# A graph network's message kernel: a row table one iteration sooner, and casts moved behind a relu

## The chip, the cores and the metric

The kernel runs on one core of a Trainium2 chip. A core has five engines that each work through a queue of their own, in order: TensorE (PE: matmuls, and PEld: the loading of their stationary operand), VectorE (DVE), ScalarE (ACT), GpSimd (POOL) and SyncE (SP, which here issues the transfers).[...] The metric is the device time of one execution in microseconds (us). TensorE writes its results to PSUM[...].

## The reference

There are 128 graphs of 64 nodes with 128 features. Each ordered pair (i, j) of nodes of a graph has a message: a three-layer MLP on the two nodes' features, with relu and layer norm after the first and the second layer. The message is multiplied by the adjacency matrix, so only pairs joined by an edge count, and the messages of a node are summed. A second MLP of the same form, on the node's features and its sum, gives the update that is added to the features.

```python
pair_feats = jnp.concatenate([f_i, f_j], axis=-1)
messages = _mlp(pair_feats, msg_w0, msg_b0, ..., msg_w2, msg_b2)
messages = messages * coupling_matrix[..., None]
agg = jnp.sum(messages, axis=2)
upd_in = jnp.concatenate([part_feats, agg], axis=-1)
updated = part_feats + _mlp(upd_in, upd_w0, upd_b0, ...)
```

About one entry of the adjacency matrix in eight is 1, and the kernel works on the edges alone.

## The kernel before, in words

**Tiling.** Each graph gets 640 slots for edges (`CAP`). Two graphs make a *pair* p (64 pairs), eight graphs a *block* b (16 blocks, `PB` = 4 pairs each), four graphs a *quarter* q of 5 chunks (32 quarters). A *chunk* n is 512 slots (160 chunks, `NCHK`), 10 to a block.

**First layer.** The first layer of the message MLP is linear in the two nodes, so the kernel computes for each node its part as the first and as the second node once (`rows`: two matmuls per graph, with `w0a` and `w0b`, into one bank; four graphs are a *half* of a block). The result is split into a rounded part and the rest: `rows_hi` (L463, ACT) casts the bank to `abh`, `rows_lo` (L469, DVE) subtracts that from the bank and writes `abl`. The bank is free when `rows_lo` is done. For each edge slot a matrix of marks S says which two nodes it joins: its upper half comes from `node_rows` (an ACT cast for pairs 2 to 5, a POOL cast for later ones, L491 and L493), its lower half from `marks` on PE and `compare` on DVE; each half is put in its place by two transfers (`stack`, L500). `node_rows` and `marks` both read the mask `tp` that `make_tp` (L484, DVE) makes of a `distance` (L478, ACT). Then `layer0` (L535) multiplies `abl` and `abh` with S, and one relu with bias on ACT (L538) empties the bank `hps` into h. There is one bank `hps`, so the next chunk's matmuls wait for that relu.

**The rest.** `stats0` turns h on PE and takes its statistics on DVE (`bn_stats`, L548). Per quarter, POOL makes the variance of five chunks (`var0_of`: L245 to L249), ACT its root (`root_of`: L255, L562), PE turns it (`turn_root`, L568). `layer1` (L602, L605) runs eight iterations after `layer0`, then a relu, statistics, and the weighted sum over edges.

**Order of the work.** Nothing schedules at run time. The program is a loop over iterations n; for each, work is registered in named places by `at(n, place, function)`, and the loop runs the places in this order: "a", "m", `layer1`, "b", `layer0`, `stats0`, "k", `stats1`, "x", "x1", "x2", "e0", "e1", "e". Each engine gets its instructions in the order in which the loop meets them. So "a" is ahead of the chunk's relu on ACT and "x" behind it.

**Around the change.** In the first iterations the pipeline is filled. Before the loop chunks 0 to 2 are done by hand, iterations 0 and 1 do `layer0` of chunks 3 and 4, iterations 2 to 4 none, and from iteration 5 on each does its own chunk. Chunks up to 4 need only the first half of block 0's rows; chunk 5 is the first to need the second, `rows(0, 1)`. Meanwhile the weights of the later layers are derived (`derivation`): each is made by an "ahead" step on ACT (L177, L200), a product on PE in a borrowed bank (L180 to L212, places "x"), and a step that empties the bank an iteration later (L184 on DVE, L193 on ACT, place "m"). The product in iteration 2 is `b1b`, the shift of the second layer. In iteration 3 place "b" `bias_table` casts it on ACT (`b1hi`, L643), and POOL builds a table from it (L645 to L649). In the same iteration, in place "e0", POOL does `var0_of` of quarter 0, and in iteration 4, place "b", ACT its root.

Borrowed banks come from `ubank` (tile `mu`, one bank: derivation in iterations 1, 2, 4, 5, 6, 7, 9 and 10, and all `rows`) and from `abank` (tile `ma`, one bank: `turn_x` in iteration 0, `count` in 1, `turn_root` in 6).

Of the kernel before, what the change touches and what calls it, by code (L numbers as in the profile page):

```python
# [23 lines left out]
def tile_gnn(  # L24
# [52 lines left out]
    PB = 4  # L77
# [207 lines left out]
    def edge_path(es):  # L285
# [18 lines left out]
        def abank():  # L304

            return ps_a.tile([P, 512], F32, name="ma")

        def ubank():

            return ps_u.tile([P, 512], F32, name="mu")  # L310
# [13 lines left out]
        def at(n, place, fn, *args):  # L324
            plan.setdefault((n, place), []).append((fn, args))
# [117 lines left out]
        def rows(b, half, k0=0, k1=4):  # L443

            blk = blocks[b]
            ps = blk["ab_ps", half] if k0 else ubank()
            for k in range(k0, k1):
                s = slice((4 * half + k) * N, (4 * half + k + 1) * N)
                nc.tensor.matmul(ps[0:N, k * C:(k + 1) * C], lhsT=blk["xnT"][:, s], rhs=w0a,
                                 start=True, stop=True)  # L450
                nc.tensor.matmul(ps[N:P, k * C:(k + 1) * C], lhsT=blk["xnT"][:, s], rhs=w0b,
                                 start=True, stop=True)
            blk["ab_ps", half] = ps
# [354 lines left out]
        for b in range(NB):  # L808
            o = b * CPB
            if b > 1:  # L810
                at(max(o - 25, 0), "a", load_adj, b)
                at(max(o - 12, 0), "a", load_x, b)
            if b > 0:
                r = max(o - 12, 1)
                at(max(o - 14, 0), "m", rank, b)
                at(r, "x", count, b)
                at(r + 1, "a", count_out, b)
                at(r + 1, "a", degrees, b)
                at(max(o - 9, r + 1), "e", place, b)
                at(*((r + 2, "a") if b == 1 else (o - 7, "e")), place_out, b)  # L820
                at(max(o - 7, 13), "m", odd_weights, b)
                at(o - 3, "x", turn_x, b)
                at(o - 2, "a", turn_x_out, b)
            for half, n in ((0, o - 2), (1, o + 3)):
                if n >= 0:
                    at(n, "x2", rows, b, half)
                    at(n + 1, "a", rows_hi, b, half)
                    at(n + 1, "m", rows_lo, b, half)
        for b in reversed(range(NB)):
            o = b * CPB  # L830
            n = o + QC + SC
# [35 lines left out]
        for p in range(NP):  # L867
            n = p * TG * 2 // CH
            if p > 1:
                if p > 2:  # L870
                    at(max(n - 7, p - 2), "a", distance, p)
                    at(max(n - 6, p - 2), "m", make_tp, p)
                at(n - 5, "a", node_rows, p)
                at(n - 4, "a", stack, p, 0, IR)
                for k in range(2):
                    at(n - 5 + k, "k", marks, p, k)
                    at(n - 5 + k, "k", compare, p, k)
                at(n - 3, "a", stack, p, 1, JR)
            w = p // 2 * QC + QC + L1 + p % 2
            last = p // 2 == NQ - 1  # L880
            at(w - 4, "a", node_marks, p)
            q, h = divmod(p, 2)
            for g in range(2):
                wait = h + 2 if q == NQ - 3 else h + 1 if q == NQ - 2 else 2 + (2 * h + g + 1) // 2
                at(*((NCHK + L1, "b") if last else (q * QC + QC + L1 + wait, "e1")), weights, p, g)
            at(NCHK + L1 + 1 if last else q * QC + SC - (q >= NQ - 3), "x1", reduce, p)
        for q in range(NQ):
            n = q * QC + QC if q else LEAD
# [35 lines left out]
        place_rest()  # L924
        bias_rows()
        rows(0, 0, 0, 2)
        rows_hi(0, 0, 0, 2)

# [17 lines left out]

        marks_here(0)
        rows(0, 0, 2, 4)
        rows_here(0, 0)
        rows_here(0, 1)  # L950
# [97 lines left out]
    with ExitStack() as es:  # L1048
        es.enter_context(tc.manual_schedule())
        flag = edge_path(es)  # L1050
# [160 lines left out]
```

## Time and profile before

| what | value |
|---|---|
| time, median of 3 runs | 575.55 us (574.04 to 575.84) |
| span of the profiled execution | 573.7 us, mean granted TensorE clock 0.983 |
| PE busy | 549.3 us (96%) |
| PEld busy | 515.0 us (90%) |
| DVE busy | 479.8 us (84%) |
| ACT busy | 476.3 us (83%) |
| POOL busy | 339.6 us (59%) |
| PE busy in 20 to 25 and 25 to 30 us | 4.01 and 2.58 us of 5 |
| PE busy in 100 to 200 us | 100.00 us of 100 |
| PE granted clock in 10 to 15, 15 to 20, 20 to 25 us | 0.50, 0.62, 1.00 |

A row of a timeline gives the start and the duration of an instruction in us, engine, line, operation, what it writes and reads, and in brackets the idle time of its engine before it with the instruction that ended it. A busy time is of the engine as a whole over the span; the stages differ, and the change lies in the first 40 us of 574.

### The profile page before, as it was taken

What the parts mean: (1) busy time and instruction counts of PE and PEld (TensorE: products, weight loads), DVE (VectorE), ACT (ScalarE), POOL (GpSimd) and SP (SyncE); (2) the same over time, 40 slices, a digit from 0 to 9 for tenths busy, and PEclk for the clock granted to TensorE, in tenths of its full rate; (3) what the DMA queues carried; (4) which work ended last, traced back from release to release, by engine and by line L of the source; (5) the groups of instructions that cost most, each with busy time, mean ns of one, the idle gap of its engine ahead of it and who ended that gap; (6) DMA issues with size and microseconds to landing.
All of it is one profiled execution on the core that took longest, in us unless ns stands there. A gap on an engine that the chain in (4) does not pass through costs nothing. (4 is left out here: it accounts for less than half of the span.)

```text
span 573.7 us, 15753 instructions
## 1 busy us (share of the span) xinstructions
PE 549.3 (96%) x5303; PEld 515.0 (90%) x5303; DVE 479.8 (84%) x1944; ACT 476.3 (83%) x1149; POOL 339.6 (59%) x898
## 2 busy tenths in 40 slices
PE   6899899999999999999999999999999999989894
PEld 4687889999999999999999999999999999979883
DVE  5768788997979899797989889798989979786686
ACT  6788979998988889898888989898888989875434
POOL 3435566665657676575757666565767656545342
PEclk7899999999999999999999999999999999998998
DMA  4464645555465545457574545546475464531201
GB/s 101 102 146 114 133 105 133 101 134 111 103 153 111 134 96 142 113 113 128 125 134 110 138 109 130 105 111 154 102 128 108 125 115 109 114 93 30 35 21 41
DMA packets 90769, 63.21 MB, mean 110 GB/s; under 512 B 57398, under 2 KB 74812, under 8 KB 90684
## 3 DMA queue, kind: packets, MB, share of 16 engines
q1 hardware_dynamic: 90396, 62.03, 49.1%
q8 instruction: 43, 0.70, 0.5%
q14 instruction: 42, 0.34, 0.2%
q10 hardware_dynamic: 288, 0.13, 0.1%
HBM read 6.82 MB, written 4.19 MB: 19 GB/s over the span
## 5 line engine op out<-in xcount | busy, mean ns | idle before, releaser
L548 DVE BATCH_NORM_STATS2 st<-hT 128x6 f32<-128x128 f32 x640 | 141.9, 284 | 36.4 <-PE hT L544 34.8
L605 PE MATMUL z<-w1c,h 128*128 128x128 f32 x1280 | 172.2, 277 | 0.0
L605 PEld LDWEIGHTS z<-w1c,h 128*128 128x128 f32 x1280 | 161.2, 192 | 8.0 <-issue 5.1
L593 ACT ACTIVATE z<-b1b,m_sd 128x128 f32<-128x128 f32 x360 | 133.6, 371 | 8.7
L615 DVE BATCH_NORM_STATS2 st<-y 128x6 f32<-128x128 f32 x640 | 137.5, 277 | 2.7 <-ACT y L608 1.4
L608 ACT ACTIVATE y<-z 128x512 f32<-128x512 f32 x160 | 94.5, 591 | 26.2 <-PE z L605 24.5
L538 ACT ACTIVATE h<-hps,b0c 128x512 f32<-128x512 f32 x160 | 109.4, 684 | 3.6 <-PE hps L535 3.3
L544 PE MATMUL hT<-ident,h 128*128 128x128 f32 x640 | 98.2, 276 | 1.5 <-DVE st L548 1.5
L678 POOL TENSOR_TENSOR w<-oh,m_q 128x320 f32<-128x320 f16 x126 | 91.9, 741 | 9.9 <-PE hT L544 5.3
L535 PE MATMUL hps<-s,abl 128*128 128x512 f32 (+3 forms) x256 | 93.2, 376 | 3.7 <-ACT h L538 2.8
L544 PEld LDWEIGHTS hT<-ident,h 128*128 128x128 f32 x640 | 76.7, 142 | 12.0 <-ACT h L538 1.3
L493 POOL CAST i<-tp 128x640 fp32r<-128x640 f16 x58 | 41.6, 718 | 68.0 <-DVE tp L484 49.1
L535 PE MATMUL hps<-s,abh 128*128 128x512 f32 (+3 forms) x256 | 79.5, 329 | 0.0
L691 PE MATMUL ys<-y,w 128*64 128x128 f32 x1280 | 76.9, 275 | 0.0
L691 PEld LDWEIGHTS ys<-y,w 128*64 128x64 f32 x1280 | 69.2, 137 | 4.2 <-issue 3.6
L245 POOL TENSOR_TENSOR m_d<-st 128x20 f32<-128x20 f32 x62 | 16.3, 263 | 88.4 <-DVE st L548 76.7
L517 DVE TENSOR_TENSOR j<-mk,cmpt 128x320 fp32r<-128x320 f32 x124 | 58.6, 473 | 1.2 <-PE mk L509 1.2
L535 PEld LDWEIGHTS hps<-s,abl 128*128 128x128 f32 x256 | 50.0, 195 | 6.2 <-ACT h L538 4.5
L478 ACT ACTIVATE d<-slot,mid 128x640 f16<-128x640 f16 x64 | 52.7, 823 | 0.0
L535 PEld LDWEIGHTS hps<-s,abh 128*128 128x128 f32 x256 | 50.3, 197 | 0.0
L469 DVE TENSOR_TENSOR abl<-mu,abh 128x512 fp32r<-128x512 f32 (+1 forms) x33 | 22.3, 675 | 31.9 <-ACT abh L463 31.7
L509 PE MATMUL mk<-tp,posall 128*128 128x320 f16 x126 | 38.0, 301 | 1.1 <-DVE tp L484 0.9
(226 smaller groups left out, 978.2 us busy)
## 6 DMA issues: line engine op xcount, KB each, us to landing
s<-i SPq DMA_DIRECT2D x124, 160.0 KB, 2.7
s<-j SPq DMA_DIRECT2D x124, 160.0 KB, 2.6
xn<-in_x_dram SPq DMA_DIRECT2D x15, 256.0 KB, 3.6
out_dram<-uo SPq DMA_DIRECT2D x15, 256.0 KB, 2.4
an<-in_adj_dram SPq DMA_DIRECT2D x16, 128.0 KB, 2.7
oh<-tp SPq DMA_TRANSPOSE x64, 3.6
xn<-in_x_dram SPq DMA_DIRECT2D x2, 128.0 KB
out_dram<-uo SPq DMA_DIRECT2D x2, 128.0 KB, 2.6
```

The lines of the kernel that those rows point to most:

```text
L478: nc.scalar.activation(D[p], slot, AF.Abs, bias=blocks[b]["mid"][:, q:q + 1], scale=-1.0)
L517: nc.vector.tensor_tensor(JR[p][:, c], MK.pop((p, k))[:, 0:HC], cmpt[:, c], op=ALU.is_equal)
L535: nc.tensor.matmul(ps[:, c:c + w], lhsT=ab[:, g % 4, :], rhs=s, start=(k == 0), stop=(k == 1))
L538: nc.scalar.activation(H[n], ps, AF.Relu, bias=b0c)
L544: nc.tensor.transpose(ps[:, t, :], H[n][:, t * P:(t + 1) * P], ident)
L548: nc.vector.bn_stats(ST0[q][:, CH * c + t, :], ps[:, t, :])
L593: nc.scalar.activation(Z[n][:, t, :], W["b1b"], AF.Copy, scale=SR[q][:, k:k + 1])
L605: nc.tensor.matmul(ps[:, t, :], lhsT=h[:, t * P:(t + 1) * P], rhs=W["w1c"], start=False, stop=True, skip_group_check=True)
L608: nc.scalar.activation(Y[n], ps, AF.Relu)
L615: nc.vector.bn_stats(ST1[q][:, CH * c + t, :], Y[n][:, t, :])
L678: (nc.vector if p == NP - 2 else nc.gpsimd).tensor_tensor(WT[p][:, :, g, :], OH[p][:, :, g * N:(g + 1) * N], Q[q][:, k:k + TG].unsqueeze(2 ...
L691: nc.tensor.matmul(YS[b][g * N:(g + 1) * N, k, :], lhsT=w[:, t, g, :], rhs=y, start=(t == 0), stop=(t == TG - 1))
```

## The change

It has three parts. The second half of rows of block 0 moves from iteration 3 to iteration 2, and with it its `rows_hi` and `rows_lo` from iteration 4 to iteration 3; as `ubank` is taken by the derivation in iteration 2, it gets the bank `abank`, free in iterations 2 to 5. The purpose is that `abh` and `abl` are there well ahead of chunk 5, and that the derivation's bank is not held by them in iteration 4. Second, the casts of pairs 2 to 5 (`node_rows`) go from place "a" to place "x" of the same iterations (0, 2, 5 and 7), that is behind the chunk's relu. Third, the `distance` of pair 4 goes from "a" to "x" of iteration 3.

```diff
-            ps = blk["ab_ps", half] if k0 else ubank()
+            ps = blk["ab_ps", half] if k0 else abank() if (b, half) == (0, 1) else ubank()
...
-            for half, n in ((0, o - 2), (1, o + 3)):
+            for half, n in ((0, o - 2), (1, o + 3 if b else 2)):
...
+                early = "x" if p < PB + 2 else "a"
                 if p > 2:
-                    at(max(n - 7, p - 2), "a", distance, p)
+                    at(max(n - 7, p - 2), "x" if p == PB else "a", distance, p)
                     at(max(n - 6, p - 2), "m", make_tp, p)
-                at(n - 5, "a", node_rows, p)
+                at(n - 5, early, node_rows, p)
```

## The prediction

> **What bounds the kernel now.** I read the table of busy time by stretch first.
>
> ```profile
> 20.00:25.00 5.00, 4.01 (x36) 3.09 (x36) 3.81 (x16) 3.72 (x13) 4.08 (x8) 1.00 0.53 129
> 25.00:30.00 5.00, 2.58 (x14) 1.73 (x14) 3.68 (x7) 3.18 (x10) 4.14 (x9) 1.00 0.52 123
> ...
> 100.00:200.00 100.00, 100.00 (x998) 95.52 (x995) 87.47 (x356) 89.10 (x218) 63.65 (x168) 1.00 0.55 121
> ```
>
> The columns after the length are busy us of PE, PEld, DVE, ACT and POOL, then the granted clock and DMA. From 100 to 200 us (and alike to 500) PE has no pause and its weight loads fill 95.5% of the time: TensorE is the bound. The change touches only iterations 0 to 8, which run from about 15 to 37 us. There PE has 1.0 + 2.4 us of idle time between 20 and 30 us. Whatever starts PE's unbroken run at 30 us earlier or later moves the end by as much, because PE then (5.00 busy of 5.00 us from 30 to 35 and from 35 to 40) has no pause before 44.6 us, and the waits after that (0.8 us before the turn of the next quarter's root) are on work that PE's own output feeds.
>
> So I looked at what PE waits for in that stretch, in PE's timeline.
>
> ```profile
> 25.82 0.49 PE L180 MATMUL mu<-wg,mean_m 128*128 128x128 f32 x2 [1.41 <-DVE abl L469]
> ...
> 26.88 0.50 PE L535 MATMUL hps<-s,abl 128*128 128x512 f32 x1
> ...
> 27.75 0.49 PE L180 MATMUL z<-wg,mean_m 128*128 128x128 f32 x2
> 29.84 0.33 PE L535 MATMUL hps<-s,abl 128*128 128x128 f32 x1 [1.59 <-ACT h L538]
> ```
>
> Two waits. At 24.4 to 25.8 PE waits for the bank of `rows(0, 1)`, which the DVE subtraction L469 frees. At 28.2 to 29.84 chunk 6's first matmul waits for chunk 5's relu (L538) to free the one bank `hps`. The second is the last before the unbroken run. So I followed that relu back on ACT.
>
> ```profile
> 22.26 0.27 ACT L193 COPY b1b<-mu 128x128 f32<-128x128 f32 x1 [0.25 <-PE mu L204]
> ...
> 22.64 0.30 ACT L643 CAST b1hi<-b1b 128x128 fp32r<-128x128 f32 x1
> ...
> 24.46 0.58 ACT L463 CAST abh<-mu 128x512 fp32r<-128x512 f32 x1 [1.03 <-PE mu L451]
> 26.83 0.31 ACT L255 ACTIVATE m_sd<-m,eps_c 128x20 f32<-128x20 f32 x1 [1.79 <-POOL m L249]
> 27.17 0.22 ACT L562 CAST sh<-m_sd 128x40 fp32r<-128x40 f32 x1
> 27.30 0.40 ACT L177 ACTIVATE wg<-u,ug1c 128x128 f32<-128x128 f32 x1
> 27.61 0.71 ACT L491 CAST i<-tp 128x640 fp32r<-128x640 f16 x1
> 28.22 0.82 ACT L478 ACTIVATE d<-slot,mid 128x640 f16<-128x640 f16 x1
> 28.95 0.24 ACT L193 COPY bu1b<-z 128x128 f32<-128x128 f32 x1
> 29.10 0.68 ACT L538 ACTIVATE h<-hps,b0c 128x512 f32<-128x512 f32 x1
> ```
>
> From 26.83 ACT runs without a break to the relu at 29.10. What starts this train is L255, which waited 1.79 us for POOL. POOL's timeline says why.
>
> ```profile
> 23.15 0.46 POOL L645 TENSOR_TENSOR b1lo<-b1b,b1hi 128x128 f32<-128x128 f32 x1
> ...
> 25.42 0.25 POOL L245 TENSOR_TENSOR m_d<-st 128x20 f32<-128x20 f32 x1
> ...
> 26.57 0.23 POOL L249 TENSOR_TENSOR m<-m_d,m_s 128x20 f32<-128x20 f32 x1
> ```
>
> POOL has no break from 23.15 to 26.80: first the bias table (L645 to L649, which needs `b1hi` of ACT), then the variance of the first quarter (L245 to L249). So the path to the start of the unbroken run is: L204 on PE, `b1b` and `b1hi` on ACT, 3.65 us of POOL, L255, and ACT's train to the relu.
>
> [...]the 1.79 us wait of L255 holds back the independent L177 and L491 behind it.[...] from the mean granted clocks (0.77 in the slice 8 to 9, 0.61 in 18 to 19, 0.71 in 515 to 520, 0.95 in 520 to 525; one half and one whole mixed) the clock drops at 8.54, returns at 18.78, drops at 517.08 and returns at 520.49[...]. Busy us of PE (second number)[...]:
>
> ```profile
> 5.13:8.54 3.41, 1.85 (x19) 1.02 (x18) 2.87 (x7) 2.69 (x6) 2.67 (x7) 1.00 0.47 110
> ...
> 22.19:25.60 3.41, 2.22 (x26) 1.73 (x24) 2.31 (x8) 1.76 (x6) 3.09 (x7) 1.00 0.80 196
> 25.60:29.02 3.42, 2.42 (x12) 1.57 (x12) 2.17 (x6) 2.16 (x6) 2.57 (x8) 1.00 0.58 137
> ```
>
> After 1.85 us (and 1.51 and 1.98 us late in the kernel) the clock was halved; after 2.22 and 2.42 us it was not.
>
> **The change, part by part.**
>
> *Casts behind the relu.* `node_rows` of pairs 2 to 5 (L491) goes from before the chunk's relu to after it. For pair 4 this takes 27.61 to 28.22 = 0.61 us out of the train ahead of the relu at 29.10: a gain of 0.61. For pair 5 the relu at 32.92 waited 0.23 us for PE anyway: 0. For pair 3 there is no relu in its iteration: 0. For pair 2 the cast filled a wait of ACT at 15.7; behind the relu of 17.23 it pushes the rest of that iteration by 0.62 (the spacing 20.26 to 20.89), so `deg` comes 0.62 later and POOL's L380 to L393 end at 23.06 + 0.62 = 23.68. The stacking transfers of these pairs start later too: pair 2's from 16.45 to about 18.6, needed only by chunk 5 at 26.9 (2.7 us to landing); pair 4's from 28.3 to about 31.5, needed by chunk 10 after 41. Hidden.
>
> *Distance of pair 4* (L478) moves behind `b1hi`. It was in an idle stretch (ACT waited 0.25 us after it). Now it delays the `wg` of L177 by 0.73, to 25.46 to 25.86. L180, which waited until 25.82 for the bank, now waits to about 25.9 for this `wg`. Net 0 or +0.08.
>
> *The second half of rows, an iteration sooner.* No instruction is added: 16 matmuls, one ACT cast, one DVE subtraction move. On PE the rows follow L208 (22.06). DVE's `make_tp` of pair 3 comes about 0.17 later, so L208 is at about 22.23, the rows run from 22.53, and end 1.09 later (23.32 to 24.41 now) at 23.62. The 1.41 us wait for L469 goes away, but nothing of it is won, as L180 waits for `wg` instead.
>
> The cast `rows_hi` (L463) is queued on ACT in place "a" of iteration 3, ahead of `b1b` and `b1hi`, which are in places "m" and "b" of that iteration. **This is the new wait.** It starts when the rows end, 23.67. Then `b1b` follows after 0.48 (38.51 to 38.98 is the same pair of forms) at 24.15, `ub0b` +0.22, `b1hi` +0.16 at 24.53, ending 24.83. Now it ends at 22.94. POOL was kept by its own L393 to 23.06, so L645 moves from 23.15 to 24.85: +1.70. The whole POOL train moves by it: L249 ends at 26.80 + 1.70 = 28.50. Could something shorten it? DVE's `bn_stats` of chunk 4 now stands behind the subtraction L469 and ends at about 25.8 instead of 24.0, still before POOL's L245 at 27.12: hidden.
>
> Sum at the relu of chunk 5: L255 at 28.53, `sh` +0.34, `wg` +0.13, distance of pair 5 +0.31, `bu1b` +0.73, relu +0.15 = 30.19. Now 29.10. So **+1.70 − 0.61 = +1.09 us**, and PE's chunk 6 starts at 30.92 instead of 29.84. Chunk 5's matmuls don't move (26.88 to about 26.95); they were never the last.
>
> The unknown size is the clock. L180 at 27.75 waits for `wg`, now at 29.40. PE's work in 25.60 to 29.02 falls from 2.42 to about 1.95 us, and any window between 25 and 32 holds 1 to 2 us. That lies at or below what halved the clock elsewhere.[...] Low end 0. But the kernel before also has a stretch with 1.82 us (26.45 to 29.86)[...], so other executions may already pay. I take 0 for the forecast and keep 0 to 2.5.
>
> **The rivals.**
> - *Halved clock* (chance 0.26): +1.09 and about 1.7: 575.55 + 2.8 = 578.3. For it: the 1.95 us above.[...]
> - *Wash* (0.16): the POOL delay is smaller than I think, or the 1.1 us is taken up by the waits for the root around 45 and 60 us. 575.6. Against: these waits follow PE's own output.
> - *Faster* (0.10): the bank wait of 1.41 and the 0.61 of the cast both come off the path, because `b1hi` has slack that I miss. 574.9 with the cast alone, 573.5 with both. For it: these are the two largest waits of PE there. Against: ACT's order is plain, and POOL shows no break between L645 and L249.
>
> **How the numbers follow.** Forecast (0.48): 575.55 + 1.09 = 576.7 us, 0.2% longer. The bound of 0.3% is 1.73 us: 573.8 to 577.3. The forecast case is inside it but for its own uncertainty (rows may end 0.3 later, a small clock loss, runs before spread 1.8 us); I give a third of it to slower, with most of the halved clock. Slower 0.40, same 0.52, faster 0.08. The range: 575.3 (most of the wash) to 578.6 (the halved clock).
>
> **What would show it.** Right: `b1hi` after `rows_hi` at about 24.5; L645 near 24.85; L255 near 28.5, still waiting for POOL; relu of chunk 5 near 30.2; L535 of chunk 6 near 30.9; no wait of L180 for L469. The stretches from 100 us on should not differ. Wrong: `b1hi` still before 23, or a shift at chunk 6 that is gone by 100 us; a granted clock under 1.00 between 25 and 40 us says the first rival.

## The result, and the profile after

The changed kernel took 579.59 us (median of four executions, 578.91 to 579.77) against 574.88 us before: **slower, ratio 1.0079, 95% interval 1.0058 to 1.0100**. A later measurement of the same kernel, with more executions on both sides, gave 579.77 against 576.49 us, ratio 1.0062 (1.0042 to 1.0082). The forecast was 576.7.

The profile after, in the same order as that of before: first PE's and the other engines' busy time by stretch (after the length: busy us of PE, PEld, DVE, ACT, POOL; then the granted clock and DMA).

```profile
25.00:30.00 5.00, 2.21 (x12) 1.27 (x10) 3.54 (x11) 1.99 (x8) 3.64 (x9) 0.96 0.53 128
30.00:35.00 5.00, 3.86 (x15) 3.33 (x16) 1.40 (x6) 3.99 (x11) 4.80 (x6) 0.50 0.27 66
35.00:40.00 5.00, 5.00 (x21) 4.23 (x21) 1.82 (x7) 2.39 (x7) 0.54 (x1) 0.51 0.48 125
100.00:200.00 100.00, 100.00 (x996) 95.37 (x995) 88.16 (x362) 89.99 (x219) 65.14 (x176) 1.00 0.55 124
```

The same stretches of the kernel before, which the prediction did not show:

```profile
30.00:35.00 5.00, 5.00 (x36) 4.40 (x37) 3.06 (x12) 3.88 (x10) 3.19 (x4) 1.00 0.44 108
35.00:40.00 5.00, 5.00 (x49) 4.62 (x48) 2.94 (x11) 4.18 (x13) 0.00 (x0) 1.00 0.74 182
```

From 100 to 200 us the two kernels are alike. From 30 to 40 us PE ran at half the clock, where before it had 1.00; PE is "busy" for 5.00 of 5.00 us from 35 to 40 in both profiles, but with 21 instructions here and 49 before: that is what half the clock looks like in a busy time. ACT's timeline shows the order that the change made:

```profile
24.27 0.58 ACT L463 CAST abh<-ma 128x512 fp32r<-128x512 f32 x1 [1.95 <-PE ma L451]
24.75 0.27 ACT L193 COPY b1b<-mu 128x128 f32<-128x128 f32 x1
24.91 0.29 ACT L193 COPY ub0b<-z 128x128 f32<-128x128 f32 x1
25.06 0.32 ACT L643 CAST b1hi<-b1b 128x128 fp32r<-128x128 f32 x1
...
29.56 0.31 ACT L255 ACTIVATE m_sd<-m,eps_c 128x20 f32<-128x20 f32 x1 [2.98 <-POOL m L249]
29.90 0.22 ACT L562 CAST sh<-m_sd 128x40 fp32r<-128x40 f32 x1
30.03 0.40 ACT L177 ACTIVATE wg<-u,ug1c 128x128 f32<-128x128 f32 x1
30.34 0.81 ACT L478 ACTIVATE d<-slot,mid 128x640 f16<-128x640 f16 x1
31.05 0.24 ACT L193 COPY bu1b<-z 128x128 f32<-128x128 f32 x1
31.20 0.68 ACT L538 ACTIVATE h<-hps,b0c 128x512 f32<-128x512 f32 x1
```

The row cast L463 now waits 1.95 us for PE at the head of iteration 3, and `b1b` and `b1hi` stand behind it. POOL's and PE's timelines show who waits for that in turn.

```profile
25.53 0.45 POOL L645 TENSOR_TENSOR b1lo<-b1b,b1hi 128x128 f32<-128x128 f32 x1 [1.43 <-ACT b1hi L643]
26.08 0.62 POOL L646 TENSOR_SCALAR b1lo<-b1lo,part 128x128 f32<-128x128 f32 x1
26.68 0.77 POOL L648 TENSOR_SCALAR b1mix<-b1hi,part 128x128 f32<-128x128 f32 x1
...
27.96 0.25 POOL L245 TENSOR_TENSOR m_d<-st 128x20 f32<-128x20 f32 x1
...
29.01 0.51 POOL L249 TENSOR_TENSOR m<-m_d,m_s 128x20 f32<-128x20 f32 x1
```

```profile
28.22 0.27 PE L212 MATMUL mu<-ident,w2c 128*128 128x128 f32 x1
30.48 0.80 PE L180 MATMUL z<-wg,mean_m 128*128 128x128 f32 x2 [1.99 <-ACT wg L177]
31.94 0.48 PE L535 MATMUL hps<-s,abl 128*128 128x128 f32 x1 [0.66 <-ACT h L538]
32.21 0.41 PE L535 MATMUL hps<-s,abh 128*128 128x128 f32 x1
32.42 0.63 PE L535 MATMUL hps<-s,abl 128*128 128x384 f32 x1
```

The `abl` matmul of 384 columns takes 0.63 us here, and took 0.39 at 30.11 before. The clock's mean of 0.81 in the slice from 29 to 30 us and 0.56 from 39 to 40 puts the half clock between 29.62 and 39.88, 10.26 us.

To split the time I measure from the relu of chunk 0, since it stands at 10.47 us in one of these profiles and at 11.11 in the other (10.47 to 11.16 in all that share this code), with nothing changed ahead of it.

| relu (L538), us after that of chunk 0 | chunk 4 | chunk 5 | chunk 8 | chunk 8 after 5 |
|---|---|---|---|---|
| before | 8.87 | 18.63 | 25.94 | 7.31 |
| after | 9.24 | 20.09 | 31.06 | 10.97 |

So the new order costs **+1.46** up to chunk 5, and the half clock **+3.66** (10.97 − 7.31) from chunk 5 to chunk 8; then the distance stays. With the 0.64 of the start, chunk 8's relu comes 5.76 us later, and so does that of every chunk up to 155. The last relu comes 4.14 later (531.82 and 535.96): the profile before lost 1.6 us to the half clock near its end (mean clock 0.86 from 510 to 520 us) and this one did not (1.00). This late fall is in five of the twelve profiles, with and without the change (before, row cast behind `b1hi`, after with pauses filled, `b1hi` late, preamble filled), and costs about 1.6 us in each (from chunk 8's relu to the end of the span it is 537.1 to 537.3 us in these five, and 535.6 to 536.3 in the others); which of the executions that were not profiled have it is not known.

### The profile page after: what moved, and what is told of

The parts are those of the page before. It is cut to its first block, busy times and chain, and to the rows that moved or that the text cites. A ratio compares the mean times of both kernels' runs of the same rounds, so it can differ in the third digit from the quotient of the medians.

```text
span 577.9 us, 15753 instructions
## 1 busy us (share of the span) xinstructions
PE 553.3 (96%) x5303; PEld 517.3 (90%) x5303; DVE 478.5 (83%) x1944; ACT 476.3 (82%) x1149; POOL 339.5 (59%) x898
## 5 line engine op out<-in xcount | busy, mean ns | idle before, releaser
L538 ACT ACTIVATE h<-hps,b0c 128x512 f32<-128x512 f32 x160 | 109.4, 684 | 5.2 <-PE hps L535 5.0
```

The lines of the kernel that those rows point to most:

```text
L538: nc.scalar.activation(H[n], ps, AF.Relu, bias=b0c)
```

## The experiments

**Theory A**: the row cast ahead of `b1hi` delays POOL's table, the first root and chunk 5's relu; PE's pause, now longer and emptier, lets the clock fall, and that is the larger part. **Rivals**: B, the casts behind the relu cost, by later transfers; C, the moved matmuls and what queues behind them cost; D, the clock is no cause. All rows of this table are of one profile each, in us after the relu of chunk 0, as above; the times are medians, with the kernel before measured beside them.

| kernel | time | before beside it | L645 starts | relu 4 | relu 5 | relu 8 after 5 |
|---|---|---|---|---|---|---|
| before | | | 12.68 | 8.87 | 18.63 | 7.31 |
| after | 579.59 | 574.88 | 14.42 | 9.24 | 20.09 | 10.97 |
| after, again | 579.77 | 576.49 | 14.86 | 9.25 | 20.53 | 12.79 |
| casts alone | 574.46 | 575.93 | 13.10 | 9.27 | 18.47 | 7.32 |
| rows alone | 580.50 | 575.93 | 15.01 | 8.63 | 21.37 | 12.79 |
| row cast behind `b1hi` | 577.50 | 575.93 | 13.07 | 9.25 | 18.30 | 8.92 |
| after, pauses filled | 577.54 | 575.93 | 14.56 | 9.26 | 20.26 | 7.34 |
| before, `b1hi` late | 580.10 | 576.42 | 14.81 | 8.62 | 20.65 | 8.84 |
| before, pauses filled | 575.27 | 576.42 | 13.03 | 9.19 | 19.04 | 7.33 |
| before, preamble filled | 576.16 | 576.42 | 11.21 | 7.39 | 17.15 | 9.24 |
| combined | 572.90 | 576.42 | 11.22 | 7.39 | 16.53 | 7.32 |
| combined, rows early | 572.63 | 576.49 | 11.18 | 7.37 | 16.41 | 7.33 |

Four kernels without a change ahead of relu 4 have it at 8.62, 8.63, 8.87 and 9.19: that much the positions differ with no change to the code ahead of them, so a difference under 0.6 in the columns up to relu 5 is not read as an effect of an edit by itself. In the three kernels with a filled preamble, filling stands ahead of relu 0 too, so the mark itself may have moved.

**The casts alone.**

```diff
-            ps = blk["ab_ps", half] if k0 else abank() if (b, half) == (0, 1) else ubank()
+            ps = blk["ab_ps", half] if k0 else ubank()
...
-            for half, n in ((0, o - 2), (1, o + 3 if b else 2)):
+            for half, n in ((0, o - 2), (1, o + 3)):
```

> The casts and the distance of pair 4 move behind the relu, the rows stay in iteration 3. Theory A (the loss comes from the row cast ahead of b1hi on ACT, and from the half clock that the longer pause of PE sets off): POOL's L645 stays within 0.6 us of 23.15, the relu of chunk 5 comes no later than before, the clock stays at 1.00 from 25 to 40 us, and the time is 574 to 575 (before is 574.9). Theory B (the casts behind the relu cost, by the later transfers of the marks): 577 or more.

574.46 us, ratio 0.9974 (0.9947 to 1.0002). In the profile the clock was 1.00 from 25 to 40 us, and relu 5 not later. (Three of the 12 executions took 577.6 to 579.5 us, as the kernel before does at times; see below.) The transfers did start later (the upper half of pair 4's marks at 30.96 instead of 28.34) and nothing waited for them. **B falls.** In ACT's timeline of this kernel L255 still waits for POOL, and the cast L491 stands behind the relu:

```profile
27.98 0.31 ACT L255 ACTIVATE m_sd<-m,eps_c 128x20 f32<-128x20 f32 x1 [1.98 <-POOL m L249]
29.63 0.69 ACT L538 ACTIVATE h<-hps,b0c 128x512 f32<-128x512 f32 x1
30.21 0.72 ACT L491 CAST i<-tp 128x640 fp32r<-128x640 f16 x1
```

From L255 to the relu it is 1.65 us instead of 2.27: the 0.61 of the cast, as the prediction had it; L255 itself came 0.46 later, counted from chunk 0.

**The rows alone.**

```diff
-                early = "x" if p < PB + 2 else "a"
+                early = "a"
...
-                    at(max(n - 7, p - 2), "x" if p == PB else "a", distance, p)
+                    at(max(n - 7, p - 2), "a", distance, p)
```

> The second half of rows moves to iteration 2 and its own bank, casts and distance stay ahead of the relu. Theory A: the row cast and then the distance of pair 4 stand ahead of b1hi, so L645 starts at about 25.6, 2.4 us later than before; the cast of pair 4 is again ahead of the relu, so that this relu comes about 2.4 later than before (about 31.5), the clock is halved[...], and the time is 580 to 582, worse than with all of the change. Theory B: near 575 or faster, as the bank wait is gone.

580.50 us, ratio 1.0070 (1.0048 to 1.0092). Relu 5 is 2.74 later than before, chunk 8 another 5.48. ACT's timeline:

```profile
23.62 0.59 ACT L463 CAST abh<-ma 128x512 fp32r<-128x512 f32 x1 [2.31 <-PE ma L451]
24.10 0.83 ACT L478 ACTIVATE d<-slot,mid 128x640 f16<-128x640 f16 x1
24.84 0.26 ACT L193 COPY b1b<-mu 128x128 f32<-128x128 f32 x1
...
25.14 0.32 ACT L643 CAST b1hi<-b1b 128x128 fp32r<-128x128 f32 x1
...
29.69 0.31 ACT L255 ACTIVATE m_sd<-m,eps_c 128x20 f32<-128x20 f32 x1 [3.74 <-POOL m L249]
```

Here the distance of pair 4 stands between the row cast and `b1b` as well, and L255 waits 3.74 us for POOL. The other two parts of the change only soften what this one does, as far as relu 5 goes (2.74 later here, 1.46 and 1.90 with all of the change); in the time the difference is within the noise (ratios 1.0070, 1.0079 and 1.0062). Here the half clock lasted longest, 17.1 us, from about 28.6 to 45.7.

**All of it, the row cast behind `b1hi`.**

```diff
-                    at(n + 1, "a", rows_hi, b, half)
-                    at(n + 1, "m", rows_lo, b, half)
+                    late = (b, half) == (0, 1)
+                    at(n + 1, "x" if late else "a", rows_hi, b, half)
+                    at(n + 1, "x" if late else "m", rows_lo, b, half)
```

> All of the change, but the row cast and the subtraction of that half go behind b1hi in the same iteration. Theory A: L645 is back at 23.7 or so (0.6 us later only, by the degrees), the relu of chunk 5 is within 0.3 us of 29.1, the clock stays at 1.00, and the time is that of before, 574 to 575.5. Theory C (it is the rows' matmuls in iteration 2, or the delay of chunk 4's transposes and statistics behind them, that cost): 578 or more.

The order is mended as A says: L645 0.39 later than before instead of 1.74, relu 5 at 18.30 against 18.63. The time was not: 577.50 us, ratio 1.0031 (1.0008 to 1.0053), outside what A expected, and its profile says why: the clock fell at 30.3 for 3.4 us, with relu 8 another 1.61 later.

```profile
28.00:30.00 2.00, 0.67 (x4) 0.30 (x2) 1.72 (x3) 1.97 (x6) 1.54 (x2) 1.00 0.74 175
30.00:31.00 1.00, 0.80 (x3) 0.80 (x4) 0.49 (x2) 1.00 (x4) 1.00 (x2) 0.65 0.01 2
31.00:33.00 2.00, 2.00 (x10) 1.76 (x10) 0.55 (x3) 1.06 (x4) 2.00 (x3) 0.50 0.56 137
```

So the kernel can lose the clock with the order of before restored, and **C does not fall here**. This kernel and the casts alone differ only by the move of the rows, and relu 5 is as early in both (18.30 and 18.47), but the medians are 577.50 and 574.46. In the two profiles 1.6 us of that is the fall at 30.3, and 1.6 the late one near the end. So moving the rows can cost something by the clock without the wrong order; how it makes a fall likelier was not found.

**All of it, PE's pauses filled.** Added are 15 matmuls on constants whose results nobody reads, ahead of the products of iterations 4 and 5 and behind the latter.

```diff
+        def fill(count):
+            ps = abank()
+            for _ in range(count):
+                nc.tensor.matmul(ps[:, 0:P], lhsT=mean_m, rhs=mean_m, start=True, stop=True)
+
+        FILLS = {2: 3, 11: 8}
...
+            if k in FILLS:
+                at(n, "x", fill, FILLS[k])
             at(n, "x", keep)
...
+        at(5, "x1", fill, 4)
```

> All of the change, and 15 matmuls on constants, whose results nobody reads, in PE's pauses of iterations 4 and 5 (3, 8 and 4 of them). Theory A: the orders on ACT and POOL stay as they are, so the relu of chunk 5 stays about 1.5 us later than before, but the clock stays at 1.00 from 25 to 40 us and the growth of the delay from chunk 5 to chunk 8 is gone: 576 to 577. Theory D (the clock is no cause, the growth comes from waits for ACT or POOL): stays at 579 to 580.

577.54 us, 0.5 above the upper end that A gave (this profile, of 577.5 us, has the late fall of 1.6 us); ratio to before 1.0014 (0.9991 to 1.0037). The late relu 5 stays (20.26, +1.63), and the growth behind it is gone: 7.34 against 7.31 before and 10.97 or 12.79 in the changed kernel. **D falls.** PE's timeline:

```profile
28.20 0.27 PE L212 MATMUL mu<-ident,w2c 128*128 128x128 f32 x1
28.31 1.95 PE L983 MATMUL ma<-mean_m 128*128 128x128 f32 x16
30.47 0.49 PE L180 MATMUL z<-wg,mean_m 128*128 128x128 f32 x2 [0.21 <-ACT wg L177]
30.80 1.06 PE L983 MATMUL ma<-mean_m 128*128 128x128 f32 x8
31.93 0.33 PE L535 MATMUL hps<-s,abl 128*128 128x128 f32 x1
```

L180 starts at 30.47 and chunk 6 at 31.93, the very times of the changed kernel (30.48 and 31.94), but they take 0.49 and 0.33 us instead of 0.80 and 0.48. The starts are the same; what differs is how long the same matmuls take.

**The kernel before with `b1hi` late**, to do the delay without any of the change:

```diff
         def bias_table():
+            ps = abank()
+            for w in (512, 512, 512, 256):
+                nc.scalar.activation(ps[:, 0:w], cmpt[:, 0:w], AF.Copy)
```

> The kernel before, rows and casts untouched, with four ACT copies of constants into a borrowed bank (three of 512 columns, one of 256, nobody reads them) ahead of b1hi, about 1.7 us. Theory A (the order of ACT ahead of b1hi, through POOL and the root, sets the start of PE's unbroken run; the clock multiplies it): L645 about 1.6 later, the relu of chunk 5 about 1.6 later against that of chunk 0 than before, the clock halved[...] between 28 and 40 us in the profile, time 579 to 581. Rival (it needs the moved rows, by the bank or PE's order): under 577.

580.10 us, ratio 1.0059 (1.0039 to 1.0078), relu 5 at 20.65. The copies held `b1hi` 2.2 us instead of the 1.7 that I had meant, and relu 5 came 2.02 later. In the profile the clock was halved for 6.8 us, from about 28.2 to 35.1.

```profile
22.65 2.29 ACT L642 ACTIVATE ma<-cmpt 128x512 f32<-128x512 f16 x4
24.88 0.28 ACT L646 CAST b1hi<-b1b 128x128 fp32r<-128x128 f32 x1
...
28.88 0.31 ACT L255 ACTIVATE m_sd<-m,eps_c 128x20 f32<-128x20 f32 x1 [2.75 <-POOL m L249]
```

The copies delay all that stands behind them on ACT, but L255 still waits for POOL, so the path is the same. Such a delay is enough; neither the rows nor the casts have to move.

**The kernel before, pauses filled** (5 and 6 such matmuls in iterations 4 and 5).

> The kernel before with 11 matmuls on constants in PE's two pauses of iterations 4 and 5. If some executions of the kernel before are halved there too (its 36 runs spread from 573.95 to 578.53), the median falls by about 1 us and the highest run goes below 577. If the spread is made elsewhere, nothing moves: 575 to 576, highest at 578.

575.27 us, ratio 0.9980 (0.9964 to 0.9996), highest 576.37. This shows what the spread of the kernel before is. Of 115 executions beside the experiments, 67 took 572.91 to 576.65 us and 48 took 577.72 to 579.78, with none between; filled, none of 20 is in the upper group. So, by its times, the kernel before also loses the clock in this stage, in four of ten executions, and its profile happened to be one of the others; no execution of the upper group was profiled.

**The kernel before, preamble filled** (3, 3, 2 and 5 such matmuls in the bank of the transposes, ahead of and between the first three chunks).

> The kernel before with 13 matmuls on constants in PE's pauses of the preamble (6 to 13 us), where the profile of before shows half the clock from 8.5 to 18.8. If PE at half the clock is on the path of the preamble, the relu of chunk 4 comes 1 to 3 us earlier against that of chunk 0, and the time falls by as much. If ACT and DVE set the pace there, nothing moves.

The clock stayed whole in the preamble (the `hps` matmuls of 256 columns took 0.37 and 0.28 us there, where they take 0.58 and 0.41 before) and relu 4 came 1.48 earlier, counted from relu 0, and at 18.74 us from the start of the span, against 19.11 to 20.43 in the kernels without this filling. So PE at half the clock was on its path. But the time did not fall with it: 576.16 us, ratio 0.9986 (0.9959 to 1.0013): in the profile the clock fell at 26.5 instead, for 6.8 us, and took 1.93 back.

```profile
20.00:25.00 5.00, 3.70 (x34) 2.96 (x34) 3.73 (x14) 3.17 (x9) 4.52 (x10) 1.00 0.57 141
25.00:30.00 5.00, 3.75 (x15) 2.68 (x16) 3.28 (x8) 3.27 (x9) 4.15 (x9) 0.65 0.60 142
30.00:35.00 5.00, 5.00 (x27) 4.35 (x27) 1.59 (x7) 2.88 (x7) 2.59 (x3) 0.66 0.24 60
```

**Combined**: both fillings (5 and 5 matmuls in iterations 4 and 5), and of the change only what the runs had shown to help, the casts of pairs 4 and 5.

```diff
-                at(n - 5, "a", node_rows, p)
+                at(n - 5, "x" if PB <= p < PB + 2 else "a", node_rows, p)
```

> The kernel before with the casts of pairs 4 and 5 alone behind the relu (pair 2 stays in ACT's wait, pair 3 and the distance stay, the rows stay), and the matmuls on constants in both stages. Theory A: the degrees are not delayed, so POOL keeps its times and the relu of chunk 5 is 0.6 earlier than before; the clock stays at 1.00 from 20 to 40 us: 572 to 574.5, below both kernels.

**572.90 us, ratio 0.9939 (0.9921 to 0.9957)**, faster than both kernels. Relu 5 is 2.10 earlier than before (1.48 from the preamble, 0.62 from the cast), and the clock is whole:

```profile
25.00:30.00 5.00, 5.00 (x38) 4.38 (x37) 4.01 (x9) 4.25 (x14) 4.84 (x6) 1.00 0.31 75
30.00:35.00 5.00, 5.00 (x49) 4.61 (x47) 2.34 (x10) 4.64 (x10) 0.87 (x1) 1.00 1.11 209
```

**Combined, with the rows early** and their cast behind `b1hi`. The `distance` of pair 4 is behind the relu here too, and the filling is of 3 and 5 matmuls in another bank.

> The combined version (casts of pairs 4 and 5 behind the relu, matmuls on constants in PE's pauses of both stages), and in addition the second half of rows in iteration 2 with its cast behind b1hi. The earlier rows free no last wait, so theory A expects 572.5 to 573.2, the same as without them (572.9) within 0.2 us. If the bank wait of 1.41 us was on the path, 571.5 or less.

572.63 us (four executions), ratio 0.9923 (0.9895 to 0.9952); relu 5 at 16.41 against 16.53. No gain of the earlier rows shows: 0.12 at relu 5 is inside the spread of the positions, and 0.27 us in the time comes from four executions. A bank wait of 1.41 us on the path would have shown. Nor do they cost anything where PE's pauses are filled, so, as far as these runs show, what C stands for costs by the clock only.

**The changed kernel again.**

> The changed kernel itself, for its spread over more executions. Theory A says that its pause of PE holds so little work that the clock is halved[...]: no execution under 578, against the kernel before, of whose executions two in three lie under 577. If it is a matter of luck as before, a part of them lies under 577 here too.

All 15 executions took 578.56 to 582.20 us, as the first four took 578.91 to 579.77. Where the kernel before loses the clock in four of ten executions, none of the 19 here is free of it, going by their times (two of them were profiled). In this profile the half clock lasted from about 30.6 to 44.3 us, 13.7 us, and took 5.48 us.

## Why the prediction was wrong, point by point

- **The path** (PE's L204, `b1b`, `b1hi`, POOL, L255, relu 5) was right, and the kernel with `b1hi` late shows it alone. **The new wait** was right: the row cast waits for PE ahead of `b1hi`, predicted at 24.53 for `b1hi`, measured at 25.06 less 0.64 of the later start = 24.42.
- **POOL's train, +1.70**: it started 1.74 later, and was longer by 0.35, as L648 took 0.77 instead of 0.62 and L249 0.51 instead of 0.23 us. L255 came 2.09 later (18.45 against 16.36).
- **The cast of pair 4, −0.61**: right (2.27 to 1.65 us from L255 to the relu).
- **The sum, +1.09 at relu 5**: 1.46 measured, the POOL term being 0.39 larger.
- **L180 waits for `wg` instead of the bank; nothing won of the 1.41 us**: right in effect; it started at 26.45 less 0.64 = 25.81, as before (25.82), just behind ACT's `wg` (25.99 to 26.40). The profile puts its wait of 1.29 us down to a transfer of marks, which landed at the same moment; L180 does not read it.
- **The clock, "I take 0 for the forecast and keep 0 to 2.5"**: **this step failed**, twice over. The measured term was 3.66 and 5.48 us. First, 1.95 us of work in 3.42 us (2.04 measured from 26.22 to 29.63, just ahead of the fall) was already at what had come ahead of a half clock elsewhere in the profile (1.85 and 1.98 us), and I had worked out that any stretch of this length between 25 and 32 us holds only 1 to 2 us. The one stretch that spoke for 0 (1.82 us of work from 26.45 to 29.86, no fall) stood against three with a fall. The forecast had to contain the term. Second, its size, 1.7 us and at most 2.5, was no more than my estimate: half of the 3.41 us at half clock from 517.08 to 520.49 is 1.7, and 2.5 is half of 5 us. The profile of before showed the clock down for 10.24 us as well, from 8.54 to 18.78, with 2.55 us of work in each of the first two stretches of 3.41 us, and I did not use that for how long it stays down. In the changed kernel PE shows as busy for all of 33.04 to 36.46 us, and the clock was at half up to 39.88 still.
- **"Other executions may already pay"**: right, four in ten. In the second comparison 8 of the 18 executions of before are in the upper group, which brings the loss in medians down to 3.3 us, below the 7.4 (1.90 and 5.48) of the profile. In the first none of the four is; there the loss is 4.7 us, and the profiles' sum of 5.1 (1.46 and 3.66) is brought down by the late fall that the kernel before had.
- The rival "halved clock" named the cause, with half its size or less (1.7 us against 3.66 and 5.48) and a chance of 0.26; "wash" and "faster" were wrong for the reasons given beside them.

## What to carry to other kernels

Ahead of moving an instruction to an earlier place of an in-order queue, ask what it waits for there and which small instruction behind it another engine needs: here a 0.3 us cast behind a 2 us wait set back POOL, ACT and PE in turn. In a stage that leaves PE partly idle, price a delay with the clock in it: sum PE's work over its pauses, and where it comes down to what stood ahead of a half clock in a profile of the same kernel (here 1.85 us in 3.41 before, 2.04 after the change), put a half clock into the forecast, not none; here it lasted 3.4 to 17.1 us and cost 1.5 to 5.5 us. Where order can't mend that, a few matmuls on constants in PE's pauses held the clock at 1.00 from 25 to 40 us here, and kept comparisons from being decided by it in that stage.

## What the runs showed of the hardware that I had not expected

- After a fall in this stage, the clock stayed at half for 3.4 to 17.1 us (3.4 with the row cast behind `b1hi`, 6.8 with `b1hi` late, 10.3 and 13.7 in the changed kernel, 17.1 with the rows alone), though PE shows as busy for most of that time (8.74 of 10.26 us in the first profile of the changed kernel). What decides how long was not found.
- PE's busy time alone doesn't tell whether the clock falls. In the changed kernel 3.41 us with 2.04 us of it were followed by the half clock, and two stretches of the same length with less were not (the first two numbers behind the length are PE and PEld):

```profile
26.22:29.63 3.41, 2.04 (x10) 1.27 (x10) 2.32 (x7) 0.43 (x3) 3.05 (x8) 1.00 0.48 115
63.76:67.18 3.42, 1.96 (x18) 1.65 (x16) 3.14 (x13) 3.01 (x9) 3.34 (x7) 1.00 0.21 56
517.74:521.15 3.41, 1.74 (x14) 1.36 (x12) 3.00 (x16) 2.97 (x8) 0.93 (x5) 1.00 0.17 37
```

  PEld, the time of the weight loads, doesn't tell by itself either: in the profile before, 3.41 us with 1.07 us of it were not followed by the half clock, and 1.27 us were in the changed kernel.

```profile
26.45:29.86 3.41, 1.82 (x10) 1.07 (x9) 2.26 (x4) 3.00 (x8) 2.65 (x5) 1.00 0.47 107
```

- In the profile of the changed kernel the clock column reads 1.00 from 10 to 15 us, while its `hps` matmuls of 256 columns take 0.58 and 0.41 us, exactly as at clock 0.50 in the profile before. Durations told the clock there, the column didn't.
